# First experts of a two-layer attention and mixture-of-experts kernel: 176 inner columns split 128 and 48, with the 48 of two blocks turned and multiplied together

## The chip, the cores and the metric

The kernel runs on one core of a Trainium2 chip. The metric is the device time of one execution in microseconds; "time before" is the median over 14 executions. All arithmetic is in float32. Five engines work side by side, each on its own list of instructions: PE (TensorE, matrix products, with its weight loads shown apart as PEld), DVE (VectorE), ACT (ScalarE), POOL (GpSimd) and SP (which only issues transfers here). A matrix product has a stationary operand, which is loaded into the array (a LDWEIGHTS record), and a moving operand, whose columns stream through it (a MATMUL record). In float32 each product is recorded as two passes, two LDWEIGHTS and two MATMUL; a transposition through PE is one pass.

## What is computed

The input x has 32 sequences of 56 rows of 256 numbers, so 1792 tokens; the context has 32 x 1500 rows of 256. Four residual layers follow one another, each on the normalised x: a decayed scan over the context whose projected mean is added and normalised; a mixture of 16 experts; an attention over the context with a mask; a mixture of two experts with 1024 inner columns. The change is in the second of them:

```python
MOE_D = 176; E = 16; K = 6
scores = softmax(h @ gate_w.T); topk_w, topk_idx = top_k(scores, K)
for e in range(E):
    g = h @ w_gate[e].T            # [T, 176]
    u = h @ w_up[e].T              # [T, 176]
    out = silu(g) * u @ w_down[e].T
    y = y + cw[:, e:e + 1] * out   # cw: the weights of the six chosen experts
```

## The kernel before

The tokens are first sorted by expert: the 1792 tokens with six experts each become at most 99 blocks (`NB0`) of 128 rows, every block with rows of one expert only. The table `ei` holds for each block where its expert's weights begin in `w0_sb`, `idx` holds which rows of the normalised input `xn0` belong to the block, and `wgt` the gate weight of each row. All weights of the 16 experts lie in SBUF as `w0_sb`, [128, 16, 1216]: for each expert two slabs of gate and up columns (one for each half of the 256 input columns, 352 columns each) and then two slabs of 256 columns for the down product. The 176 inner columns are cut into two halves of 88 (`H0`), so each down slab fills partitions 0 to 87. `w0_down_pieces` (lines 188 to 203) yields the transfers that put the down weights there, 26 in all; they are issued on SP during the first layer.

`expert_blocks` (lines 704 to 772) serves both mixtures: the 99 blocks of the first with one unit each (`nq` = 1), and later the 15 blocks of the second with four units each. It is a software pipeline over t, written out by hand, and its order is the order of each engine's list (the schedule is manual for all engines in this stage). In iteration t:

1. `gate_up(t)`: two products of the turned rows `xT[t]` with the gate and up columns of the block's expert, 352 columns wide, into a PSUM tile `gu` (line 720); PE reads the expert's offset from `ei` first (line 715). Then ACT computes silu of the gate half into `sg` (line 726), and DVE multiplies it by the row's gate weight and by the up half into `hs` (line 732).
2. `turn(t-1)`: two transpositions of `hs`, 88 columns each, into a PSUM tile `tp` (line 738); DVE copies both to `hT` (line 740).
3. `turned_rows` for block t+1: two transpositions of the gathered rows `xb` (line 166), and a copy on ACT to `xT` (line 168). The rows were gathered by POOL four blocks ahead (line 865).
4. `down(t-2)`: two products of `hT` with the two down slabs, 256 columns wide, summed in a PSUM tile `y` (line 747); then `done` copies `y` on ACT to `yb` (line 873) and sends it from SP to the table `ys0` in HBM (line 874).
5. `side(t)`: small work of the neighbouring layers. For t from 2 to 21 three DVE instructions each that work out where each token's results will lie (lines 889 to 904); five context loads of 1.5 MB and five zero fills on SP; gathers of finished rows on POOL; and in four iterations four transpositions on PE for the first queries of the attention (line 840).

So gate-up of iteration t+1 needs the `xT` copied in iteration t, and the work of step 4 stands between the two in PE's list. The PSUM tiles have two buffers each, the SBUF tiles `sg`, `hs`, `hT`, `xT` and `yb` three.

After the stage, the attention begins. It scores with line 1027, whose operands use 32 partitions each, and sums with line 1075.

Of the kernel before, what the change touches and what calls it, by code (L numbers as in the profile page):

```python
# [8 lines left out]
F32 = mybir.dt.float32  # L9
# [45 lines left out]
def xattn_ffn_kernel(  # L55
# [132 lines left out]
    def w0_down_pieces():  # L188

        half = E0 // 2  # L190
        for e in range(half):
            for c in range(2):
                r = 0
                while r < H0:
                    f = e * F0 + c * H0 + r
                    n = min(H0 - r, P - f % P)
# [504 lines left out]
        V.tensor_copy(wgt, bl[:, P : P + NB0])  # L701
        V.tensor_copy(ei, ep[0:1, 0:P])

    def expert_blocks(nb, nq, f, w, ei, wk, ptr, pgu, pht, py, rows_of, done, ahead, wgt=None, side=None):

        fp = f // nq
        h = fp // 2
        doff = 2 * KD * fp
        piece = doff + 2 * D
        units = [(i, u) for i in range(nb) for u in range(nq)]  # L710
        xT, at, hs, hT, y = {}, {}, {}, {}, {}

        def gate_up(i, u):
            if u == 0:
                at[i] = PE.value_load(
                    ei[0:1, i : i + 1], min_val=0, max_val=w.shape[1] - nq * piece
                )
            gu = pgu.tile([P, 512], F32, tag="gu", name="gu")
            for k in range(KD):
                PE.matmul(  # L720
                    gu[:, 0 : 2 * fp], lhsT=xT[i][:, k, :],
                    rhs=w[:, bass.ds(at[i] + (u * piece + k * 2 * fp), 2 * fp)],
                    start=(k == 0), stop=(k == KD - 1),
                )
# [4 lines left out]
            if wgt is None:  # L729
                V.tensor_tensor(hs[i, u], sg, up, ALU.mult)  # L730
            else:
                V.scalar_tensor_tensor(hs[i, u], sg, wgt[:, i : i + 1], up, ALU.mult, ALU.mult)  # L732

        def turn(i, u):
            tp = pht.tile([P, 512], F32, tag="ht", name="tp")
            a = hs.pop((i, u))
            for c in range(2):
                PE.transpose(tp[0:h, c * P : (c + 1) * P], a[:, c * h : (c + 1) * h], ident)  # L738
            hT[i, u] = wk.tile([h, 2 * P], F32, tag="hT", name="hT")
            V.tensor_copy(hT[i, u], tp[0:h, 0 : 2 * P])  # L740

        def down(i, u):
            if u == 0:
                y[i] = py.tile([P, 512], F32, tag="y", name="y")
            a = hT.pop((i, u))
            for c in range(2):
                PE.matmul(  # L747
                    y[i][:, 0:D], lhsT=a[:, c * P : (c + 1) * P],
                    rhs=w[0:h, bass.ds(at[i] + (u * piece + doff + c * D), D)],
                    start=(u == 0 and c == 0), stop=(u == nq - 1 and c == 1),  # L750
                )
# [5 lines left out]
        if side:  # L757
            side(-1)
        for t in range(len(units) + 2):
            if t < len(units):  # L760
                gate_up(*units[t])
            if 0 <= t - 1 < len(units):
                turn(*units[t - 1])
            if t < len(units) and units[t][1] == nq // 2 and units[t][0] + 1 < nb:
                i = units[t][0] + 1
                if i + ahead - 1 < nb:
                    xb[i + ahead - 1] = rows_of(i + ahead - 1)
                xT[i] = turned_rows(wk, ptr, "tr", xb.pop(i))
            if t >= 2:
                down(*units[t - 2])  # L770
            if side:
                side(t)

    def levels_of(p):

# [74 lines left out]
    with tc.manual_schedule(  # L850
# [113 lines left out]
    with tc.manual_schedule(  # L964
# [255 lines left out]
        def turn(p, n):  # L1220
            return [transposed(2 * p + h, n) for h in range(2)]
# [77 lines left out]
    with tc.tile_pool(name="f1", bufs=3) as wk, tc.tile_pool(  # L1299
        name="f1_tr", bufs=2, space=PSUM  # L1300
    ) as ptr, tc.tile_pool(name="f1_gu", bufs=2, space=PSUM) as pgu, tc.tile_pool(
        name="f1_ht", bufs=2, space=PSUM
    ) as pht, tc.tile_pool(name="f1_y", bufs=2, space=PSUM) as py:
        last = NP - GP

        def side1(t):

            if t == -1:
                roots(mvs[NP - 1])
                sort_norm(NP - 1, mvs.pop(NP - 1))  # L1310
# [23 lines left out]
        expert_blocks(  # L1334
            NB1, NQ1, F1, w1_sb.rearrange("p e w -> p (e w)"), e1i,
            wk, ptr, pgu, pht, py, lambda i: xb1[i][:, 0:D], done1, 1, None, side1,
        )


# [54 lines left out]
```

## Time and profile before

| what | value |
|---|---|
| median of 14 executions | 894.48 us (891.03 to 907.58) |
| the profiled execution: its time, its span | 901.24 us, 899.5 us |
| mean granted TensorE clock | 0.948 |
| PE busy | 811.7 us, 90% of the span |
| DVE, ACT, POOL busy | 483.9, 343.3, 398.0 us |
| first experts, 209.70 to 462.40 us | PE busy 251.67 of 252.70 us, DVE 92.03, ACT 109.42, POOL 138.63 |
| attention, 466.80 to 704.10 us | PE busy 212.12 of 237.30 us, DVE 187.20 |
| second experts, 717.00 to 895.00 us | PE busy 174.27 of 178.00 us |

The stage times are read from windows of the trace. A row of the timeline gives the start, the length, the engine, the line, the operation and the operands' names and shapes; "88*128" is 88 rows (partitions) by 128 columns of the stationary operand. Equal instructions that touch are merged into one row, with their count behind x. The end of a matrix pass is modelled by the profiler, and passes overlap: what a pass really takes is seen from the distance between starts. Queue rows (SPq, PEldq) are instructions that only issue or read a register.

### The profile page before, as it was taken

To read this page: it belongs to the slowest core of one execution; us is meant where nothing else is said; L and a number is where in the kernel's file an instruction comes from. 1 tells how busy PE (TensorE), PEld (TensorE's weight loads), DVE (VectorE), ACT (ScalarE), POOL (GpSimd) and SP (SyncE) were. 2 spreads that over 40 slices of the span, in tenths; PEclk is the share of its full clock that TensorE was granted. 3 is DMA by queue.
4 is the path that set the end of the run, shared out by engine and by line. 5 is a ranking of instruction groups with operands and counts; after the bars stand their busy time and mean duration, and the time that the engine had idled before them with its cause. 6 is when DMAs were issued, how large, how long until landed. Compare 5 with 4: busy or idle time off the path is not lost.

```text
span 899.5 us, 18673 instructions
## 1 busy us (share of the span) xinstructions
PE 811.7 (90%) x6664; PEld 531.8 (59%) x6664; DVE 483.9 (54%) x1420; ACT 343.3 (38%) x901; POOL 398.0 (44%) x479
## 2 busy tenths in 40 slices
PE   4688788788999999999988999988959989999997
PEld 3345555545777777777754666555635556666664
DVE  3577777862552424322257989868739333333222
ACT  0233333312444444444435776746536321111110
POOL 4555655434347656575624655565540330111110
PEclk9799999958999999999988999998989999999999
DMA  8999999922987534344537988796963820011110
GB/s 250 351 390 384 379 368 355 305 65 74 313 295 247 161 106 141 101 141 116 125 106 249 305 273 279 244 309 232 320 232 93 274 83 13 25 35 30 35 31 17
DMA packets 77820, 176.58 MB, mean 196 GB/s; under 512 B 7795, under 2 KB 41476, under 8 KB 77732
## 3 DMA queue, kind: packets, MB, share of 16 engines
q1 hardware_dynamic: 64756, 139.55, 44.8%
q0 software_dynamic: 12976, 35.85, 14.2%
q8 instruction: 56, 0.92, 0.4%
q14 instruction: 32, 0.26, 0.1%
HBM read 150.83 MB, written 25.20 MB: 196 GB/s over the span
## 4 chain that ended last, share of the span: by engine, by line
PE 46%; POOL 11%; DMA 9%; issue 6%; DVE 3%; ACT 1%; POOLq 0%; DVEq 0%; ACTq 0%
PE gu L720 23%; PE y L747 14%; DMA g<-ys,back 8%; POOL g L782 6%; PE tp L738 4%; PE tp L166 3%; POOL g L792 2%; PE op L1075 1%; DVE cT L988 1%; POOL g L793 1%; POOL g L794 1%; DMA xs<-pay,to 1%; PE sp L1027 1%; POOL xr L795 1%; POOL xs L1166 0%
## 5 line engine op out<-in xcount | busy, mean ns | idle before, releaser
L720 PE MATMUL gu<-w_sb,xT 128*128 x396 | 136.3, 466 | 2.1 <-DMA xb<-xn,idx 1.1
L726 ACT ACTIVATE sg<-gu 128x176 f32<-128x176 f32 (+1 forms) x159 | 54.4, 343 | 216.9 <-PE gu L720 216.9
L865 POOL DMA_INDIRECT xb<-xn,idx x99 | 93.8, 947 | 91.8 <-PE tp L166 74.6
L732 DVE SCALAR_TENSOR_TENSOR hs<-sg,wgt,gu 128x176 f32<-128x176 f32 x99 | 39.3, 397 | 160.0 <-ACT sg L726 153.9
L720 PE MATMUL gu<-ring,xT 128*128 x240 | 114.3, 600 | 0.5 <-ACT xT L168 0.5
L782 POOL DMA_INDIRECT g<-ys,back x96 | 91.2, 950 | 33.3 <-issue 26.4
L747 PE MATMUL y<-w_sb,hT 88*128 x396 | 101.8, 379 | 0.0
L1027 PE MATMUL sp<-cT,xq 32*64 32x384 f32 x2048 | 94.1, 512 | 3.4 <-DVE cT L988 3.3
L720 PEld LDWEIGHTS gu<-w_sb,xT 128*128 128x128 f32 x396 | 75.0, 191 | 30.2 <-ACT xT L168 3.2
L730 DVE TENSOR_TENSOR hs<-sg,gu 128x256 f32<-128x256 f32 x60 | 25.2, 421 | 117.1 <-ACT sg L726 117.1
L738 PEld LDWEIGHTS tp<-ident,hs 128*88 128x88 f32 (+1 forms) x318 | 41.2, 130 | 62.9 <-issue 48.6
L988 DVE STREAM_TRANSPOSE cT<-ring 128x1536 f32<-128x1536 f32 x40 | 69.2, 1758 | 15.1 <-PE sp L1027 10.0
L1075 PE MATMUL op<-ring,pT 128*64 128x256 f32 x480 | 67.7, 396 | 9.4 <-issue 9.3
L1329 POOL DMA_INDIRECT out<-ob,ti x15 | 14.8, 989 | 130.9 <-DVE ob L1326 130.6
L1027 PEld LDWEIGHTS sp<-cT,xq 32*64 32x64 f32 x2048 | 45.7, 139 | 44.0 <-issue 17.5
L747 PEld LDWEIGHTS y<-w_sb,hT 88*128 88x128 f32 x396 | 67.3, 190 | 5.6 <-issue 0.2
L168 ACT COPY xT<-tp 128x256 f32<-128x256 f32 x130 | 48.4, 372 | 51.5 <-PE tp L166 50.6
L740 DVE COPY hT<-tp 88x256 f32<-88x256 f32 (+1 forms) x159 | 66.0, 415 | 0.7 <-PE tp L738 0.6
L720 PEld LDWEIGHTS gu<-ring,xT 128*128 128x128 f32 x240 | 45.6, 191 | 33.2 <-issue 29.5
L738 PE MATMUL tp<-ident,hs 128*88 128x128 f32 (+1 forms) x318 | 61.1, 274 | 2.6 <-DVE hs L730 2.6
L1075 PEld LDWEIGHTS op<-ring,pT 128*64 128x64 f32 x480 | 41.6, 142 | 36.9 <-issue 17.2
L747 PE MATMUL y<-ring,hT 128*128 x240 | 61.7, 380 | 0.0
(264 smaller groups left out, 1342.2 us busy)
## 6 DMA issues: line engine op xcount, KB each, us to landing
ring<-in_cx SPq DMA_DIRECT2D x52, 1536.0 KB
extra<-in_cx SPq DMA_DIRECT2D x12, 1536.0 KB
ys<-yb SPq DMA_DIRECT2D x99, 128.0 KB
xs<-zrow SPq DMA_DIRECT2D x5, 771.0 KB
mu<-in_mask SPq DMA_DIRECT2D x16, 187.5 KB
w_sb<-in_wg SPq DMA_DIRECT2D x2, 1408.0 KB
w_sb<-in_wu SPq DMA_DIRECT2D x2, 1408.0 KB
xn<-xn SPq DMA_DIRECT2D x16, 128.0 KB
```

The costliest lines, as they stand in the source:

```text
L168: A.copy(xT.rearrange("p k c -> p (k c)"), tp[:, 0 : KD * P])
L720: PE.matmul(gu[:, 0 : 2 * fp], lhsT=xT[i][:, k, :], rhs=w[:, bass.ds(at[i] + (u * piece + k * 2 * fp), 2 * fp)], start=(k == 0), stop=(k = ...
L726: A.activation(sg, gu[:, 0:fp], AF.Silu)
L732: V.scalar_tensor_tensor(hs[i, u], sg, wgt[:, i : i + 1], up, ALU.mult, ALU.mult)
L738: PE.transpose(tp[0:h, c * P : (c + 1) * P], a[:, c * h : (c + 1) * h], ident)
L740: V.tensor_copy(hT[i, u], tp[0:h, 0 : 2 * P])
L747: PE.matmul(y[i][:, 0:D], lhsT=a[:, c * P : (c + 1) * P], rhs=w[0:h, bass.ds(at[i] + (u * piece + doff + c * D), D)], start=(u == 0 and c ...
L782: G.indirect_dma_start(out=g[:, k, :], out_offset=None, in_=ys0[0 : n * P, :], in_offset=bass.IndirectOffsetOnAxis(ap=back[:, p, 3 * i + k ...
L865: G.indirect_dma_start(out=xb, out_offset=None, in_=xn0, in_offset=bass.IndirectOffsetOnAxis(ap=idx[:, i : i + 1], axis=0),)
L988: V.transpose(out=cT.rearrange("p j e q -> p j (e q)"), in_=slots[b % NS][:, :, P * n : P * n + P],)
L1027: PE.matmul(sps[a][64 * h : 64 * h + 64, 0 : Q * NCH], lhsT=xq[Q * a : Q * a + Q, e, 64 * h : 64 * h + 64], rhs=cTs[e // 4][h][Q * a : Q * ...
L1075: PE.matmul(op[64 * h : 64 * h + 64, 0:D], lhsT=pT[:, j, 64 * h : 64 * h + 64], rhs=slots[(2 * p + h) % NS][:, j, :], start=(j == 0), stop ...
```

## The change

The 176 inner columns are now split 128 and 48 (`R0`). The first down slab fills all 128 partitions, the second only partitions 0 to 47; the pieces that load them become 25. The first mixture gets a pipeline of its own, `first_blocks`; `expert_blocks` loses its weight argument and serves only the second.

In `first_blocks` DVE writes the weighted product in two instructions: 128 columns to `hs` and 48 to `rest`. One `rest` tile belongs to two successive blocks: the even block's 48 columns stand at column 0, the odd block's at column 64, with zeros (written once by POOL) between. `turn` transposes `hs` for every block; after an odd block it also transposes the 112 columns of `rest`, so that the even block's part lands on partitions 0 to 47 and the odd block's on 64 to 111, copied to `h2`. `down` of an even block makes only the product over its 128 rows. `down` of an odd block makes its own product over 128 rows, then one of 48 rows for the even block, from partition 0, and one of 48 rows for itself, from partition 64; then both blocks are done. The weights for the partitions from 64 are a copy of the odd block's second slab: SP reads the expert's offset and sends 48 KB from `w0_sb` to a tile `w2`, four blocks ahead of the block's gate-up. Block 98 has no partner and makes its 48-row product alone.

```diff
-H0 = F0 // 2
+R0 = F0 - P
+    def first_blocks(w, wk, ptr, pgu, pht, py, rows_of, done, ahead, side):
+        rest = [wk.tile([P, 64 + R0], F32, tag=f"rest{i}", bufs=1, name="rest") for i in range(3)]
+        def gate_up(i):
...
+            b = 64 * (i % 2)
+            for dst, o, n in ((hs[i], 0, P), (rest[i // 2 % 3][:, b : b + R0], P, R0)):
+                V.scalar_tensor_tensor(
+                    dst, sg[:, o : o + n], wgt[:, i : i + 1], gu[:, F0 + o : F0 + o + n],
+                    ALU.mult, ALU.mult,
+                )
+        def pair(i):
+            if i % 2 == 0 and i < NB0 - 1:
+                return []
+            return [(j, 64 * (j % 2)) for j in range(i - i % 2, i + 1)]
+        def rest_of_weights(i):
+            r = nc.sync.value_load(ei[0:1, i : i + 1], min_val=0, max_val=w.shape[1] - W0)
+            w2[i] = wk.tile([P, D], F32, tag="w2", bufs=4, name="w2")
+            nc.sync.dma_start(
+                out=w2[i][64 : 64 + R0, :], in_=w[0:R0, bass.ds(r + (2 * KD * F0 + D), D)]
+            )
+        def turn(i):
+            tp = pht.tile([P, 512], F32, tag="ht", name="tp")
+            PE.transpose(tp[:, 0:P], hs.pop(i), ident)
+            n = 64 * len(pair(i)) - 64 + R0
+            if pair(i):
+                PE.transpose(tp[0:n, P : 2 * P], rest[i // 2 % 3][:, 0:n], ident)
+            h1[i] = wk.tile([P, P], F32, tag="h1", name="h1")
+            V.tensor_copy(h1[i], tp[:, 0:P])
+            if pair(i):
+                h2[i] = wk.tile([P, P], F32, tag="h2", bufs=2, name="h2")
+                V.tensor_copy(h2[i][0:n, :], tp[0:n, P : 2 * P])
+        def down(i):
+            y[i] = py.tile([P, 512], F32, tag="y", name="y")
+            PE.matmul(
+                y[i][:, 0:D], lhsT=h1.pop(i), rhs=w[:, bass.ds(at[i] + 2 * KD * F0, D)],
+                start=True, stop=False,
+            )
+            for j, b in pair(i):
+                PE.matmul(
+                    y[j][:, 0:D], lhsT=h2[i][b : b + R0, :],
+                    rhs=w2.pop(j)[b : b + R0, :] if b
+                    else w[0:R0, bass.ds(at[j] + (2 * KD * F0 + D), D)],
+                    start=False, stop=True,
+                )
+            for j, _ in pair(i):
+                done(j, y.pop(j))
+        for i in (1, 3):
+            rest_of_weights(i)
+        for r in rest:
+            G.memset(r[:, R0:64], 0.0)
+        xT[0] = turned_rows(wk, ptr, "tr", xb.pop(0))
+        for t in range(NB0 + 2):
+            if t < NB0:
+                gate_up(t)
+                if t % 2 and t + 4 < NB0:
+                    rest_of_weights(t + 4)
+            if 0 < t <= NB0:
+                turn(t - 1)
+            if t + 1 < NB0:
...
+                xT[t + 1] = turned_rows(wk, ptr, "tr", xb.pop(t + 1))
+            if t >= 2:
+                down(t - 2)
+            side(t)
...
-        expert_blocks(
-            NB0, 1, F0, w0_sb.rearrange("p e w -> p (e w)"), ei,
-            wk, ptr, pgu, pht, py, rows_of, done, 4, wgt, side,
+        first_blocks(
+            w0_sb.rearrange("p e w -> p (e w)"), wk, ptr, pgu, pht, py, rows_of, done, 4, side,
         )
```

More of the change, by code (lines that the diff above doesn't have):

```diff
@@ L193, in w0_down_pieces @@
                 r = 0
-                while r < H0:
-                    f = e * F0 + c * H0 + r
-                    n = min(H0 - r, P - f % P)
+                while r < (R0 if c else P):
+                    f = e * F0 + c * P + r
+                    n = min((R0 if c else P) - r, P - f % P)
                     o = 2 * KD * F0 + c * D
@@ L702, in xattn_ffn_kernel @@
         V.tensor_copy(ei, ep[0:1, 0:P])
-    def expert_blocks(nb, nq, f, w, ei, wk, ptr, pgu, pht, py, rows_of, done, ahead, wgt=None, side=None):
+    def first_blocks(w, wk, ptr, pgu, pht, py, rows_of, done, ahead, side):
+        xT, at, hs, h1, h2, w2, y = {}, {}, {}, {}, {}, {}, {}
+        rest = [wk.tile([P, 64 + R0], F32, tag=f"rest{i}", bufs=1, name="rest") for i in range(3)]
+        def gate_up(i):
+            at[i] = PE.value_load(ei[0:1, i : i + 1], min_val=0, max_val=w.shape[1] - W0)
+            gu = pgu.tile([P, 512], F32, tag="gu", name="gu")
+            for k in range(KD):
+                PE.matmul(
+                    gu[:, 0 : 2 * F0], lhsT=xT[i][:, k, :],
+                    rhs=w[:, bass.ds(at[i] + k * 2 * F0, 2 * F0)],
+                    start=(k == 0), stop=(k == KD - 1),
+                )
+            sg = wk.tile([P, F0], F32, tag="sg", name="sg")
+            A.activation(sg, gu[:, 0:F0], AF.Silu)
+            hs[i] = wk.tile([P, P], F32, tag="hs", name="hs")
+            b = 64 * (i % 2)
[32 more added lines that the diff above has]
+            for j, b in pair(i):
+                PE.matmul(
+                    y[j][:, 0:D], lhsT=h2[i][b : b + R0, :],
+                    rhs=w2.pop(j)[b : b + R0, :] if b
+                    else w[0:R0, bass.ds(at[j] + (2 * KD * F0 + D), D)],
+                    start=False, stop=True,
+                )
+            for j, _ in pair(i):
+                done(j, y.pop(j))
+        xb = {i: rows_of(i) for i in range(ahead)}
+        for i in (1, 3):
[11 more added lines that the diff above has]
+            if t + 1 < NB0:
+                if t + ahead < NB0:
+                    xb[t + ahead] = rows_of(t + ahead)
+                xT[t + 1] = turned_rows(wk, ptr, "tr", xb.pop(t + 1))
+            if t >= 2:
+                down(t - 2)
+            side(t)
@@ L706, in expert_blocks @@
+    def expert_blocks(nb, nq, f, w, ei, wk, ptr, pgu, pht, py, rows_of, done, ahead, side):
         fp = f // nq
@@ L728, in gate_up @@
             up = gu[:, fp : 2 * fp]
[L729 to L732, printed above, removed]
+            V.tensor_tensor(hs[i, u], sg, up, ALU.mult)
         def turn(i, u):
@@ L756, in expert_blocks @@
         xT[0] = turned_rows(wk, ptr, "tr", xb.pop(0))
-        if side:
-            side(-1)
+        side(-1)
         for t in range(len(units) + 2):
@@ L770, in expert_blocks @@
                 down(*units[t - 2])
-            if side:
-                side(t)
+            side(t)
     def levels_of(p):
@@ L1335, in xattn_ffn_kernel @@
             NB1, NQ1, F1, w1_sb.rearrange("p e w -> p (e w)"), e1i,
-            wk, ptr, pgu, pht, py, lambda i: xb1[i][:, 0:D], done1, 1, None, side1,
+            wk, ptr, pgu, pht, py, lambda i: xb1[i][:, 0:D], done1, 1, side1,
         )
```

## The prediction

> **What bounds the kernel now.** I read the page's costliest groups first, then windows over the stage, then the chain of waits inside it, then one iteration engine by engine.
>
> ```profile
> L720 PE MATMUL gu<-w_sb,xT 128*128 x396 | 136.3, 466 | 2.1 <-DMA xb<-xn,idx 1.1
> L747 PE MATMUL y<-w_sb,hT 88*128 x396 | 101.8, 379 | 0.0
> ```
>
> The two products of the stage are among PE's largest groups, and PE hardly idles before them. A window of 60 us in mid-stage has PE busy all the time at full clock:
>
> ```profile
> 300.00:360.00 60.00, 60.00 (x298) 45.70 (x297) 22.49 (x77) 28.78 (x76) 37.33 (x40) 1.00 0.45 132
> ```
>
> (Columns: PE, PEld, DVE, ACT, POOL, clock, DMA share, GB/s.) The chain gives one iteration as the bare sum of PE's passes:
>
> ```profile
> 264.43 1.19 PE gu L720 x4
> 265.61 0.22 PE tp L738 x2
> 265.83 0.22 PE tp L166 x2
> 266.05 0.86 PE y L747 x4
> 266.91 1.19 PE gu L720 x4
> ```
>
> 1.19 + 0.22 + 0.22 + 0.86 = 2.49 us a block: a gate-up pass takes 0.296, a transposition 0.11, a down pass 0.216. But a second path has the same length. The timelines of PE, PEld and ACT over the same iteration (here by start of record):
>
> ```profile
> 264.26 1.35 PE L720 MATMUL gu<-w_sb,xT 128*128 x4
> 265.67 0.38 PE L166 MATMUL tp<-ident,xb 128*128 128x128 f32 x2
> 265.88 1.03 PE L747 MATMUL y<-w_sb,hT 88*128 x4
> 266.14 0.37 ACT L168 COPY xT<-tp 128x256 f32<-128x256 f32 x1 [0.17 <-PE tp L166]
> 266.56 0.97 PEld L720 LDWEIGHTS gu<-w_sb,xT 128*128 128x128 f32 x4
> 266.75 1.35 PE L720 MATMUL gu<-w_sb,xT 128*128 x4
> ```
>
> The row transpositions start 1.41 after the gate-up. From there to the next gate-up's weight load are 0.89 (265.67 to 266.56): transpose, hand over to ACT, copy 0.37, hand back. ACT idles 0.17 before the copy, so it is latency, not load. The load of 0.19 ends at 266.75, exactly when the four down passes are through. The down passes cover the turning of the next block's rows, with almost nothing to spare.
>
> **The change, part by part**, per pair of blocks, against 2 x 2.487 = 4.974.
>
> *Removed.* One transposition in four: -0.11, in the odd iteration (it turns an even block). The down passes stay eight of 256 columns per pair: four over 128 rows, four over 48.
>
> *Moved.* The even block's second product goes to the next iteration. So iterations with t even run two down passes after the row transpositions, 0.43 instead of 0.87, and PE then waits for `xT`. What is late next is that copy: 1.41 + 0.89 = 2.30 to the load, and the load's own share in front of the first pass. Upper bound of that share 0.19, its recorded length; a lower one comes from line 473 below, where four 16-column passes with a load each go by in 0.55, so at most 0.14 together; I take 0.10. Even iteration 2.40, -0.09. Two down passes fewer therefore bring a fifth of their 0.43.
>
> *Added.* Two 48-row products from partitions 0 and 64. Can they run at once? The trace of before has no 64-row operands, but line 1027 has 32-row ones, into separate PSUM tiles as here, and line 435 has a 3-row one between 128-row neighbours:
>
> ```profile
> 510.20 5.42 PE L1027 MATMUL sp<-cT,xq 32*64 32x384 f32 x128
> 515.55 0.43 PE L1075 MATMUL op<-ring,pT 128*64 128x256 f32 x1
> ...
> 102.70 0.62 PE L473 MATMUL lp<-gw_sb,xT 128*128 128x16 f32 x4 [0.46 <-ACT xT L168]
> 103.25 0.69 PE L435 MATMUL bp<-sm,takes 3*128 3x256 f32 x2
> 103.87 0.64 PE L294 MATMUL acc<-ring,cz 128*32 128x256 f32 x8
> ...
> 26.33 1.10 PE L332 MATMUL vp<-wout_sb,bcol 128*128 128x256 f32 x4 [0.60 <-DVE t L345]
> 27.36 0.69 PE L336 MATMUL vp<-bout_sb,ones 1*128 1x256 f32 x2
> 27.99 0.27 PE L348 MATMUL tk<-ident,t 128*3 128x128 f32 x1
> ```
>
> 128 passes of 384 columns pass in 5.35 us, 0.042 each; a lone one would take 0.216 x 384/256 = 0.32. So eight tiles of the array work together, and both passes of each: I take the two products as concurrent, 0.43 for four passes. But each change of tile shape costs. Line 435's two passes hold the array 0.62 to the next group, line 336's 0.63, where two down passes take 0.43: 0.19 to 0.20 more, a gap of some 0.09 and an uncovered load of 0.10 for one change. Neighbouring lines of equal shape (720, 738, 166, 747) show no gap. The pair changes shape twice, into the 48-row products and back to gate-up: 2 x 0.19 = 0.38. So 0.43 + 0.38 = 0.81 stands where four passes took 0.87. Bounds: 0.43 (no price) to 0.87 + 0.38 = 1.25 (not concurrent).
>
> The Trainium skill, page "TensorE: Matmul & The Clock Gate", Part 3, prices packed tiles at one product's duration plus some 4 ns for each further tile and lets a load for another row group overlap running products; by that the four passes would cost 0.43 and the sum below would be a gain of about 9 us. Its page "TensorEngine Tiling (Array Packing)", Key Properties, says that changing the mode drains the engine, without a price; the rows of lines 435 and 336 side with this one.
>
> Odd iteration: 1.19 + 0.11 + 0.22 + 0.43 + 0.81 = 2.76, +0.27. Its `xT` is ready after 1.19 + 0.11 + 0.89 = 2.19, well before.
>
> *Other engines.* DVE writes two pieces instead of one (397 ns for 176 columns; each piece between 0.14, its smallest rows, and 0.40) and copies 128 columns per block and again per pair (413 ns for 256; about half each). That is 0.2 to 0.5 us more per iteration. Around 240 us, with the three side instructions, DVE still idles 0.76 per iteration before line 732, and iterations do not get shorter than 2.40; `hs` has over an iteration until it is turned. Nothing. ACT makes the two `yb` copies of a pair together, 0.74, at the start of the even iteration; silu waits for gate-up's end 1.39 in. Nothing. They use the three `yb` buffers faster; before, ACT waited for one transfer once, 0.9 us. SP gets 49 more loads of the offset (PE's takes 0.30 to 1.15) and 48 KB transfers, before the `ys` issues and context loads of their iteration; SP's largest waits are for ACT's `yb` (219.7 us), and a weight copy has six iterations, 14 us, while gathers of 128 KB land in 2.7 to 5.4. Bounds 0 to 1 us in all, taken as 0. POOL's three small fills come after the first four gathers, and 25 pieces replace 26: nothing.
>
> *Sum.* Pair -0.09 + 0.27 = +0.18; 48 pairs with a following gate-up: +8.8 (0.184 unrounded). The query transpositions (line 840, 0.44 us after the down passes) fall twice into an even iteration's hole of 0.3: -0.6. The last blocks drop four-pass groups and add three changes of shape: +0.2. Total **+8.5 us**. What follows the stage starts from its last `ys0` block and moves with it. The profiled execution took 901.24 for a span of 899.5, 0.8% above the median 894.48; its iterations of 2.49 at full clock have no reason to differ in other executions, so I add to both: 909.7 for a profile like this one, **903** for the median.
>
> **The rivals.**
>
> *A. As above, slower by about 1%.* For it: lines 435, 336 and the equal lengths of the two paths. Between 899 and 910, from 0.1 to 0.33 a pair.
>
> *B. Faster: 64-row tiles join without a price.* The weight loads overlap and no gap opens. Odd iteration 1.95 + 0.43 = 2.38; pair 2.40 + 2.38 = 4.78, -0.19; 48 pairs -9: **885**. It decides once a change costs under 0.095 us (half the 0.19 of line 435). For it: no 64-row operand was seen. Against it: every change of shape above, from 1 to 32 rows and in both directions.
>
> *C. The two products don't run together.* The change then does not do what it says. Odd iteration +0.43: pair +0.61, 48 pairs +30: **924**; with only one pass of each overlapped +0.40, +19: **914**. For it: each product's two passes stand next to each other in PE's list. Against it: so they do in line 1027.
>
> *D. No change.* A change costs about 0.10, say because the load is hidden and only the gap stays: pair about 0: **895**.
>
> **How the numbers follow.** A 0.64, B 0.15, C 0.11, D 0.10. The time is A's, 903. About 0.5%, 4.5 us, is what a measurement of this kernel can tell from no change: 890 to 899. A's low edge touches that. Faster: B, 0.15 and a little of D, so 0.17; same: 0.08 of D and 0.05 of A, 0.13; slower: 0.70. The range has to hold 8 in 10: A and D, and half of C and B's edge: 889 to 914. A's own is 899 to 910.
>
> **What would show it.** In the profile after: PE's weight load of `gu` waits for ACT's `xT` some 48 times, 0.3 to 0.4 each, where before it did so 4 times; iterations alternate, 2.40 and 2.76; the 48-row products are two pairs of simultaneous passes, 0.32 and 0.22 long, with about 0.3 between the last 128-row pass and the first of them instead of 0.22; the stage takes about 261 us instead of 252.7. Alternating 2.40 and 2.38 is B; 48-row passes in single file are C. Wrong altogether I would be if DVE or the 48 KB copies held PE back, which would show as waits of lines 738 or 747.

## The result, and the profile after

| | before | after |
|---|---|---|
| median | 895.58 us (889.94 to 907.58, 47 executions) | 904.83 us (902.82 to 914.59, 10 executions) |
| the profiled execution: time, span, clock | 901.24, 899.5, 0.948 | 901.80, 900.1, 0.961 |
| first gate-up of the first experts to the issue of the last `ys0` block | 209.7 to 462.8: 253.1 us | 208.9 to 469.2: 260.3 us |

The changed kernel is slower: ratio 1.0122, 95% interval 1.0098 to 1.0147, the medians 9.25 us apart. (Here and below the medians are over all executions, and the ratios leave out those in a slower state.) The two profiled executions must not be subtracted: the one of before lay 0.6% above its median and the one of after 0.3% below, and the attention, which the change doesn't touch, took 236.7 us from its first to its last scores instruction in the one and 232.8 in the other, with the clock's half-speed stretches at other places. The stage itself can be compared, and it is 7.2 us longer.

The costliest groups of the stage, after (line, engine, operation, operands, count; then busy time and the mean of one in ns; then idle time before them and what ended most of it):

```profile
L714 PE MATMUL gu<-w_sb,xT 128*128 x396 | 144.4, 487 | 4.6 <-ACT xT L168 2.0
L714 PEld LDWEIGHTS gu<-w_sb,xT 128*128 128x128 f32 x396 | 67.6, 190 | 60.4 <-ACT xT L168 23.1
L757 PE MATMUL y<-w_sb,h 128*128 x198 | 59.3, 381 | 0.5 <-ACT yb L956 0.5
```

The gate-up's weight load now idles 60.4 us before it starts, and 23.1 of that ends with ACT's copy of `xT`. PE shows little idle time of its own, since a load record and the modelled end of the pass before it cover the gap. The waits of the stage name it directly (us in total, times, longest), first in the kernel before:

```profile
PEld gu L720 <- ACT xT L168: 3.2, 4, 1.3
```

and after:

```profile
PEld gu L714 <- ACT xT L168: 23.1, 47, 1.5
PEld gu L714 <- issue: 16.6, 50, 0.4
PEld y L762 <- issue: 16.2, 49, 0.3
...
ACT yb L956 <- DMA ys<-yb: 2.2, 2, 1.7
```

47 gate-ups wait for `xT`, mostly for 0.43 us, where four did before. In the other iterations, some 50 times each, the load before the first 48-row product and the load before the gate-up that follows idle 0.3 "for issue", that is for nothing the profile names: these two start 0.31 after the start of the last pass before them, where the load of a 128-row pass starts while the pass before it runs. The chain of waits through one odd and one even iteration (start, length, what):

```profile
264.29 1.45 PE gu L714 x4
265.74 0.11 PE tp L745
265.85 0.22 PE tp L166 x2
266.07 0.43 PE y L757 x2
266.50 0.63 PE y L762 x4
267.13 1.38 PE gu L714 x4
268.51 0.11 PE tp L745
268.62 0.11 PE tp L748
268.73 0.22 PE tp L166 x2
268.95 0.43 PE y L757 x2
269.38 0.03 issue
269.41 1.45 PE gu L714 x4
```

Where before had one repeated sum of PE's passes, a hand-over ("issue", after the wait for ACT) now sits in every second iteration, and the gate-up's four passes are put down as 1.38 and 1.45 in place of 1.19, because the chain counts in an uncovered load among them (0.10) and the idle stretch ahead of them. In the timelines of PE, PEld and ACT the same stretch shows where each pass and load begins:

```profile
265.90 0.60 PE L757 MATMUL y<-w_sb,h 128*128 x2
266.43 0.48 PE L762 MATMUL y<-w_sb,h 48*128 x1
266.44 0.48 PE L762 MATMUL y<-w,h 48*128 48x256 f32 x1
266.75 0.38 PE L762 MATMUL y<-w_sb,h 48*128 x1
266.76 0.38 PE L762 MATMUL y<-w,h 48*128 48x256 f32 x1
267.06 1.45 PE L714 MATMUL gu<-w_sb,xT 128*128 x4
...
267.06 0.89 PEld L714 LDWEIGHTS gu<-w_sb,xT 128*128 128x128 f32 x4 [0.33 <-issue]
...
269.41 0.59 PEld L714 LDWEIGHTS gu<-w_sb,xT 128*128 128x128 f32 x3 [0.43 <-ACT xT L168]
...
268.99 0.37 ACT L168 COPY xT<-tp 128x256 f32<-128x256 f32 x1
```

The two 48-row products start 0.01 apart, and so do their second passes: they do run together. But the first of them begins 0.31 after the last 128-row pass instead of 0.22, the second pair 0.32 after the first, and the gate-up 0.31 after the second. In the even iteration the load of the gate-up starts at 269.41, 0.05 after the copy that ended at 269.36. An iteration is from here on the distance between the starts of two gate-ups' first passes: 267.06 to 269.41, 2.35 us, is the even one; the odd one before it took 2.77. Over the whole stage the medians are 2.349 and 2.775, so 5.124 a pair against 4.976 before.

The stage's 7.2 us can be added up from the starts of all gate-ups and the end: 48 pairs at +0.148 are +7.1; two even iterations (t = 10 and t = 16) were longer by 1.0 together; the four iterations with query transpositions, and the two that follow them, took 1.06 more than normal instead of 1.76, -0.7; the end, from the last gate-up to the last `ys0` issue, took 6.3 instead of 5.1, +1.2; and the first pair took 5.80 instead of 7.16, -1.4. That is +7.2. The last term is the clock's and not the change's: in the profile of before the second gate-up, too, ran at half speed (granted clock 0.53 from 213 to 216 us, against 1.00 from 212.4 to 214 us in the profile after).

```profile
213.32 2.68 PE L720 MATMUL gu<-w_sb,xT 128*128 x4 [0.46 <-ACT xT L168]
```

```profile
212.43 1.45 PE L714 MATMUL gu<-w_sb,xT 128*128 x4 [0.46 <-ACT xT L168]
```

These rows of the timelines of before and of after are the gate-up of t = 1. Without that accident the stage would be 8.6 us longer, close to the distance of the medians. The ratio's interval, 8.8 to 13.2 us of 895.58, begins just above that and allows up to 4.6 us more; where that would lie, I did not find.

### The profile page after: what moved, and what is told of

Its sections match the earlier page's. It is cut to its first block, busy times and chain, and to the rows that moved or that the text cites. A ratio compares the mean times of both kernels' runs of the same rounds, so it can differ in the third digit from the quotient of the medians.

```text
span 900.1 us, 18919 instructions
## 1 busy us (share of the span) xinstructions
PE 808.9 (90%) x6615; PEld 494.8 (55%) x6615; DVE 489.8 (54%) x1569; ACT 339.1 (38%) x901; POOL 398.7 (44%) x482
## 4 chain that ended last, share of the span: by engine, by line
PE 50%; issue 5%; DVE 5%; POOL 5%; DMA 4%; ACT 2%; POOLq 0%; DVEq 0%
PE gu L714 13%; PE gu L808 9%; PE sp L1109 5%; PE y L832 5%; PE op L1157 4%; PE y L757 4%; PE y L762 3%; DMA g<-ys,back 3%; DVE cT L1070 2%; PE tp L166 2%; POOL g L865 2%; PE tp L1149 1%; PE tp L823 1%; PE tp L745 1%; DVE sc L1122 1%
## 5 line engine op out<-in xcount | busy, mean ns | idle before, releaser
L714 PE MATMUL gu<-w_sb,xT 128*128 x396 | 144.4, 487 | 4.6 <-ACT xT L168 2.0
L724 DVE SCALAR_TENSOR_TENSOR hs<-sg,wgt,gu 128x128 f32<-128x128 f32 x99 | 34.4, 348 | 158.7 <-ACT sg L720 150.9
L714 PEld LDWEIGHTS gu<-w_sb,xT 128*128 128x128 f32 x396 | 67.6, 190 | 60.4 <-ACT xT L168 23.1
L814 ACT ACTIVATE sg<-gu 128x256 f32<-128x256 f32 x60 | 22.9, 384 | 138.1 <-PE gu L808 138.1
L720 ACT ACTIVATE sg<-gu 128x176 f32<-128x176 f32 x99 | 31.5, 318 | 110.4 <-PE gu L714 106.2
L757 PE MATMUL y<-w_sb,h 128*128 x198 | 59.3, 381 | 0.5 <-ACT yb L956 0.5
L875 POOL TENSOR_TENSOR g<-g 128x768 f32<-128x768 f32 x16 | 29.2, 1828 | 61.0 <-DMA g<-ys,back 60.9
L294 PE MATMUL acc<-ring,cz 128*32 128x256 f32 x768 | 54.2, 440 | 0.3 <-DVE cz L270 0.3
L544 POOL TENSOR_SCALAR oh<-iota,off 128x128 f32<-128x128 f32 x64 | 39.7, 634 | 16.4 <-DVE off L520 14.1
```

What stands on the lines that cost most here:

```text
L294: PE.matmul(acc[Q * g : Q * g + Q, 0:D], lhsT=cz[:, j, 1 - h : 1 - h + Q], rhs=c[:, j, :], start=(h == 0 and m == 0), stop=(h == 1 and m = ...
L544: G.tensor_scalar(oh[:, i, :], iota, off[:, i : i + 1], None, ALU.is_equal)
L714: PE.matmul(gu[:, 0 : 2 * F0], lhsT=xT[i][:, k, :], rhs=w[:, bass.ds(at[i] + k * 2 * F0, 2 * F0)], start=(k == 0), stop=(k == KD - 1),)
L757: PE.matmul(y[i][:, 0:D], lhsT=h1.pop(i), rhs=w[:, bass.ds(at[i] + 2 * KD * F0, D)], start=True, stop=False,)
```

## The experiments

Three of the chips on which the experiments ran took 967 to 970 us for the kernel before, a fourth 964, not 895, and there PE, ACT and DVE stop for some microseconds five times in this stage (last section). The whole times below therefore carry these stops. Their cost is given as the time that the iterations from the first to the last gate-up take above their normal length, added up: 27 to 49 us, against 4 and 3 us in the two profiles of the first chip, where nothing stops. What an edit does to the work is read from the median length of the iterations, which agrees to 0.002 us between kernels and chips wherever the same work is done.

My theory: the pair is longer because (a) the even iteration, freed of two passes, runs into the wait for `xT`, and (b) the joint products pay two changes of tile shape. The rivals: the joint products are not joint, or the loss comes from the new DVE instructions, the weight copies or `yb`.

**Rows turned earlier, in the changed kernel** (rows_two_ahead). If the hole is the wait for `xT`, it closes when the rows are turned two iterations ahead.

```diff
-        xT[0] = turned_rows(wk, ptr, "tr", xb.pop(0))
+        for i in range(2):
+            xT[i] = turned_rows(wk, ptr, "tr", xb.pop(i))
...
-            if t + 1 < NB0:
-                if t + ahead < NB0:
-                    xb[t + ahead] = rows_of(t + ahead)
-                xT[t + 1] = turned_rows(wk, ptr, "tr", xb.pop(t + 1))
+            if t + ahead < NB0:
+                xb[t + ahead] = rows_of(t + ahead)
+            if t + 2 < NB0:
+                xT[t + 2] = turned_rows(wk, ptr, "tr", xb.pop(t + 2))
...
-            w0_sb.rearrange("p e w -> p (e w)"), wk, ptr, pgu, pht, py, rows_of, done, 4, side,
+            w0_sb.rearrange("p e w -> p (e w)"), wk, ptr, pgu, pht, py, rows_of, done, 5, side,
```

> The changed kernel, but each block's rows are turned two iterations before their gate-up instead of one (five gathers ahead instead of four), so the copy to xT is never awaited. Theory (even iterations have a hole while the copy is awaited, and the changes of tile shape use up what the joint 48-row products save): the even iteration falls from 2.35 to its passes, 1.19 + 0.22 + 0.22 + 0.43 = 2.06, the odd one stays 2.78; pair 4.84 against 5.12, 48 pairs -14 us against the changed kernel, so about 5 us faster than the kernel before (ratio 0.993 to 0.996). Rival (the loss is DVE's, ACT's or SP's added work, or the changes of shape alone): no gain, ratio stays at 1.012.

Measured: even 2.159, odd 2.671, a pair 4.83. The chain of waits, from the end of an even iteration through an odd one:

```profile
258.80 0.43 PE y L757 x2
259.24 1.18 PE gu L714 x4
260.42 0.11 PE tp L745
260.53 0.22 PE tp L166 x2
260.75 0.43 PE y L757 x2
261.18 0.63 PE y L762 x4
261.81 1.38 PE gu L714 x4
```

There is no "issue" any more, the gate-up after an even iteration's products is back at 1.18, and only the one after the 48-row products keeps 1.38. So the hole is worth 5.124 - 4.830 = 0.294 a pair, in the two forms of a late load (0.19 in the even iteration) and an uncovered one (0.10 in the odd). The whole time, 968.52 us, is 1.0024 of before on the same chip (0.9978 to 1.0071): the gain of 7 us that 49 pairs at -0.146 would make does not show. The stops took 40 us here, and 32 us on the same chip in before_rows_two_ahead (below), whose iterations are those of the kernel before. A difference of this size would hide the gain, but the kernel before itself has no trace on this chip.

**The same beside the changed kernel** (rows_two_ahead_again, changed_again). To weigh the hole in time, both ran on one chip.

> The changed kernel with its rows turned two iterations ahead, a second time: in the first run its iterations were 2.16 and 2.67, pair 4.83 as expected, but on that chip every engine stopped together for some 8 us about every 40 us, in the kernel before as well, so that the time couldn't be told. Theory, without such stops: 48 x 0.29 = 14 us faster than the changed kernel, ratio to before 0.993 to 0.996. Rival: 1.012 as the changed kernel.

> The changed kernel itself, beside the others on the same chip. Ratio 1.010 to 1.015; iterations 2.35 and 2.78.

Measured: 969.12 us (1.0037 of before, 0.9992 to 1.0083) with the rows turned earlier; the changed kernel as it is 984.93 (1.0184, 1.0117 to 1.0251), with the same 2.349 and 2.775 as on the first chip. The stops were equal in the two, 40.0 and 40.4 us, so the 15.8 us between them can be set against the hole, 49 x 0.294 = 14.4. The expectation for the changed kernel (1.010 to 1.015) was too low; the stops were longer than those of the two kernels made from before (27 and 32 us, on another chip).

**Rows turned earlier, in the kernel before** (before_rows_two_ahead). If that edit were a gain by itself, the reading above would be worth less. The same lead of two iterations in `expert_blocks`, for the first mixture alone, again with five gathers ahead:

```diff
-        xT[0] = turned_rows(wk, ptr, "tr", xb.pop(0))
+        lead = 2 if nq == 1 else 1
+        for i in range(lead):
+            xT[i] = turned_rows(wk, ptr, "tr", xb.pop(i))
...
-                xT[i] = turned_rows(wk, ptr, "tr", xb.pop(i))
+                i += lead - 1
+                if i < nb:
+                    xT[i] = turned_rows(wk, ptr, "tr", xb.pop(i))
...
-            wk, ptr, pgu, pht, py, rows_of, done, 4, wgt, side,
+            wk, ptr, pgu, pht, py, rows_of, done, 5, wgt, side,
```

> The kernel before with the same early turning of the rows in the first experts. Theory: PE's passes alone already fill its iterations of 2.487, so nothing moves, ratio 0.998 to 1.002. Rival (turning the rows early is a gain of its own, whatever the change): faster by as much as the changed kernel with it.

Measured: every iteration 2.488, and 965.37 us, 1.0020 of before (0.9971 to 1.0069). In the kernel before nothing waits for `xT`, as predicted; the path has the length of the passes and no more.

**The hole alone** (before_moved). The kernel before with nothing changed but the place of the even block's second product: still 88 rows, no shape changes, no weight copies, no further DVE instructions.

```diff
-            for c in range(2):
+            late = nq == 1 and i % 2 == 0 and i < nb - 1
+            todo = [(i, 0)] if late else [(i, 0), (i, 1)]
+            if nq == 1 and i % 2:
+                todo = [(i, 0), (i - 1, 1), (i, 1)]
+            for j, c in todo:
...
-            if u == nq - 1:
-                done(i, y.pop(i))
+            if u == nq - 1 and not late:
+                for j in ([i - 1, i] if nq == 1 and i % 2 else [i]):
+                    done(j, y.pop(j))
...
```

> The kernel before (176 = 88 + 88, all as it was), but the second down product of an even block is made in the next iteration, so that iterations have two and six down passes in turn. PE's passes are the same. Theory: the even iteration waits for xT, 2.35 to 2.40 instead of falling to 2.05, the odd one is 2.49 + 0.43 = 2.92; pair 5.27 to 5.32 against 4.97, 49 pairs +15 to +17 us, ratio 1.016 to 1.019. Rival (the waiting for xT is covered, moving passes costs nothing): ratio 1.000.

Measured: even 2.248, odd 3.022, a pair 5.27, +0.294: the same figure that the rows turned earlier gave back. The even iteration is 0.10 shorter and the odd one 0.10 longer than expected, since from start to start the uncovered load behind the hole counts to the odd one. 985.15 us, 1.0153 of before (1.0028 to 1.0279). The chain has the same hand-over without any 48-row product:

```profile
257.40 0.03 issue
257.42 1.45 PE gu L720 x4
...
259.31 1.30 PE y L751 x6
260.61 1.19 PE gu L720 x4
```

So moving work out of the iteration is the whole of (a). In the changed kernel the joint products and the dropped transposition then give back 0.146 of it.

**The 48-row products without a change of shape** (whole_shape_rest). Both products over 112 rows, with the partner's rows of the weights filled with zeros, so the array keeps its whole shape and the two can't run together.

```diff
+        for lo, hi in ((32, 64), (64, P)):
+            G.memset(w0_sb[lo:hi, :, 2 * KD * F0 + D : W0], 0.0)
...
+        N = 64 + R0
...
-                    y[j][:, 0:D], lhsT=h2[i][b : b + R0, :],
-                    rhs=w2.pop(j)[b : b + R0, :] if b
-                    else w[0:R0, bass.ds(at[j] + (2 * KD * F0 + D), D)],
+                    y[j][:, 0:D], lhsT=h2[i][0:N, :],
+                    rhs=w2.pop(j)[0:N, :] if b
+                    else w[0:N, bass.ds(at[j] + (2 * KD * F0 + D), D)],
...
+        for i in range(4):
+            V.memset(w2s[i][0:64, :], 0.0)
```

> The changed kernel, but its two 48-row products are made over 112 rows, with zeros in the weights for the partner's rows, so that no tile shape changes and nothing runs together: four passes in a row. Theory: the odd iteration is 1.19 + 0.11 + 0.22 + 0.43 + 0.87 = 2.82 instead of 2.78, the even one stays 2.35: 2 us slower than the changed kernel, ratio to before 1.013 to 1.016; joining the products with its two changes of shape is worth only 0.04 us a pair. Rival (the changes of shape are the loss): back to the kernel before, ratio 1.000.

Measured: even 2.248, odd 2.914, a pair 5.16; 983.49 us, 1.0144 of before (1.0026 to 1.0262). The pair is what was expected (2.35 + 2.82), with 0.10 of it in the other iteration: no change of shape puts an uncovered load into the even one.

```profile
256.40 0.43 PE y L762 x2
256.83 0.87 PE y L767 x4
257.70 1.19 PE gu L719 x4
```

Four passes in single file take 0.87 and the gate-up behind them 1.19, where the joint ones take 0.63 with a gate-up of 1.38 behind them. 0.87 + 1.19 = 2.06 against 0.63 + 1.38 = 2.01: running the two products at once brings 0.04 to 0.05 us a pair, not the 0.43 of two passes. The two changes of shape take the rest, 0.39, so 0.19 each.

**Both products from one row group** (one_row_group). The opposite bound: the changed kernel with both 48-row products on partitions 0 to 47. It leaves out the odd block's rest, so its result is not the layer's; only its times are used.

```diff
-                    y[j][:, 0:D], lhsT=h2[i][b : b + R0, :],
-                    rhs=w2.pop(j)[b : b + R0, :] if b
-                    else w[0:R0, bass.ds(at[j] + (2 * KD * F0 + D), D)],
+                    y[j][:, 0:D], lhsT=h2[i][0:R0, :],
+                    rhs=w[0:R0, bass.ds(at[j] + (2 * KD * F0 + D), D)],
```

> The changed kernel, but both 48-row products read partitions 0 to 47, so they can't run together; the odd block's rest is thereby left out and the even block's multiplied in its place. The changes of tile shape stay. Theory (the two products of the changed kernel do run together): four passes in a row, the odd iteration 2.78 + 0.43 = 3.21, the even one 2.35, pair 5.56, 49 pairs 21 us slower than the changed kernel, ratio to before about 1.035. Rival (they never ran together, or it doesn't matter): the same as the changed kernel.

Measured: even 2.350, odd 3.200; 1002.01 us, 1.0314 of before (1.0247 to 1.0380). The timeline of PE:

```profile
230.52 1.13 PE L762 MATMUL y<-w_sb,h 48*128 x4
231.57 1.15 PE L714 MATMUL gu<-w_sb,xT 128*128 x3
```

The four passes now begin at 230.52, 230.84, 231.05 and 231.27, and the gate-up 1.06 after the first of them, where with the joint ones it begins 0.63 after. The odd iteration is 0.425 longer, two passes of 0.216: this is what the second row group saves. The pair, 5.549, is 0.388 longer than the 5.161 of whole_shape_rest, which makes the same number of passes in single file: that is the price of the two changes of shape, with no joining in it. The rival "not joint" is out.

**Balanced, whole shape** (balanced_whole_shape). Each block's rest, over 112 rows, in the next block's iteration, so that every iteration has four down passes again and the one transposition in four is still saved. The edit is shown against whole_shape_rest.

```diff
-            for j, b in pair(i):
+            todo = ([(i - 1, 64 * ((i - 1) % 2))] if i else []) + ([(i, 0)] if i == NB0 - 1 else [])
+            for j, b in todo:
                 PE.matmul(
-                    y[j][:, 0:D], lhsT=h2[i][0:N, :],
+                    y[j][:, 0:D], lhsT=h2[min(j | 1, NB0 - 1)][0:N, :],
...
-            for j, _ in pair(i):
+            for j, _ in todo:
                 done(j, y.pop(j))
```

> The changed kernel with its 48-row products made over 112 rows (weights padded with zeros, so no change of tile shape), and each block's product made in the iteration of the next block, so that every iteration has four down passes, as before. Theory: no hole and no change of shape; what stays of the change is one transposition in four: 2.38 and 2.49, pair 4.87 against 4.97 before, 49 pairs -5 us, ratio 0.993 to 0.996. Rival (the turning of the rest, its copies on DVE, and the weight copies by SP cost something by themselves): ratio 1.000 or more.

Measured: 2.489 and 2.381, a pair 4.87, as expected: the hole is gone without turning rows earlier, and the saved transposition (0.11) is all that is left of the change. The time missed its expectation: 978.86 us, 1.0150 of before (1.0084 to 1.0216), and the stops took 48 us.

**Five `yb` buffers** (two_ahead_buffers). Two even iterations of the changed kernel were longer because ACT waited for the transfers out of `yb`; the stops might have been the same thing. The rows turned earlier, with five `yb` buffers in place of three (and, not shown here, two `rest` tiles and three `w2` to make room):

```diff
-            yb = wk.tile([P, D], F32, tag="yb", name="yb")
+            yb = wk.tile([P, D], F32, tag="yb", bufs=5, name="yb")
```

> The changed kernel with its rows turned two iterations ahead and five instead of three buffers for yb (paid for by two instead of three tiles for the rest and three instead of four for the copied weights, fetched two blocks ahead). The iterations stay 2.16 and 2.67, and ACT no longer waits for the transfers of yb, which in the changed kernel lengthened two iterations by 1.0 us together. On the two chips of the earlier runs everything stopped five times in this stage, each time as the second half of a token group's results was being gathered. If those stops come from ACT's wait for yb, they shrink, and the ratio to before falls below 0.993; if they don't, it stays at 1.002 to 1.004 on such a chip, and 0.993 to 0.996 on one without stops.

Measured: iterations unchanged (2.158, 2.671), the stops still 36.5 us, 977.06 us, 1.0058 of before (1.0004 to 1.0111). In this stage ACT no longer waits for a transfer out of `yb`, where with three buffers it did so five times for 6.9 us in all (rows_two_ahead). The stops are not a lack of `yb` buffers.

**One change of shape for four blocks** (groups_of_four, and twice more on other chips). If 0.38 a pair goes into changes of shape, joining four blocks' 48-row products halves it. Blocks i and i+2 share a bank of PSUM, ACT copies two blocks at once, the rows are turned two iterations ahead.

```diff
-            y[i] = py.tile([P, 512], F32, tag="y", name="y")
+            if i % 4 < 2:
+                y[i] = py.tile([P, 512], F32, tag="y", name="y")
+            else:
+                y[i] = y[i - 2]
+            o = D * (i % 4 // 2)
...
-            for j, b in pair(i):
+            if i % 4 < 3 and i < NB0 - 1:
+                return
+            for j in range(i - i % 4, i + 1):
+                b = 64 * (j % 2)
+                o = D * (j % 4 // 2)
...
```

> Rows turned two iterations ahead, and the 48-row products collected over four blocks: two pairs at a time, one after the other, so that two changes of shape serve four blocks. PSUM: the products of blocks i and i+2 share a bank, ACT copies two blocks at once, the transposed rows have one bank. Theory: four blocks take 4 x 1.185 + 8 x 0.109 + 6 x 0.109 + 8 x 0.2165 + 4 x 0.2165 + 0.38 = 9.24 against 9.95 before; 24.5 groups -17 us, ratio 0.980 to 0.984, if nothing else becomes the bound; in the first 20 iterations DVE, with some 2.2 us of work per iteration, may. Rival (changes of shape cost nothing, only the hole did): no better than the rows turned ahead alone, 0.994.

> The groups of four again, in the hope of a chip without the stops. In the earlier run its iterations outside of them took 9.26 us for four blocks (9.24 expected, 9.95 before), but the stops took 16 us more than with the kernel before and its rows turned early. Without stops: 17 us faster than before, ratio 0.980 to 0.984. With them: 1.00 to 1.01 as before.

> The same kernel as groups_of_four, on whatever chip comes. Its four iterations together take 9.26 us at full clock, against 9.95 before (4 x 2.488); 24 such groups make 16.6 us less. If the chip is one on which the kernel before takes about 895 us and the stage has no stops of all engines, the time should be 0.980 to 0.985 of before. If the stops of 5 to 10 us are there as on the chips of the other runs (before at 967 to 970 us), they should cost this kernel some 49 us against some 33 before and take the gain away: 1.003 to 1.014.

Measured: the four iterations 2.054, 3.103, 2.158 and 1.945, together 9.26, on all three chips, against 9.95 before. The chain at the 48-row products:

```profile
261.72 0.43 PE y L761 x2
262.15 1.06 PE y L770 x8
263.22 1.38 PE gu L714 x4
```

Eight passes in 1.06 where two pairs of four take 1.26, and one gate-up of 1.38 for four blocks instead of two: the price of a change of shape is paid per visit, not per product. In time it lost on every chip: 971.82 us, 1.0051 (1.0003 to 1.0099); 983.19, 1.0131 (1.0078 to 1.0184); 971.65, 1.0077 (1.0040 to 1.0113). The stops took 48 to 49 us. So no version was faster than the kernel before in a measurement; that this one would where the stops are absent, by some 16 us (0.69 for each of 24 groups), is worked out from its iterations and was not measured.

## Why the prediction was right, point by point

**Forecast and result.** 903 was said, 904.83 came, and A, the likeliest case, is what happened. The sum of +8.5 stands against +7.2 in the profiled stage, +8.6 without the half-speed gate-up of before, and +9.25 between the medians. Some of that agreement is luck: the pairs cost 1.7 us less than said, the `yb` waits and the end 2.0 us more.

**Even iteration, said 2.40, measured 2.349.** The mechanism was right: 47 waits for ACT's `xT` were found where 48 were forecast. The term that was mis-sized is the 0.89 from the first row transposition to the next gate-up's load: it took 0.84 (268.57 to 269.41), because ACT's copy began 0.42 after the transposition and not 0.47. It did so in nearly all even iterations, and 0.47 after in the odd ones; why, the runs don't show. The 0.10 for a load was right in size and stands in another place. The first pass is recorded as starting with its load, so the load behind the hole falls to the odd iteration (0.40 between the first two passes from 269.41, instead of 0.295). The even iteration has the like at its own start, after the change of shape (267.06 to 267.46): without shape changes it is 2.248, with them 2.349.

**Odd iteration, said 2.76, measured 2.775.** The 0.81 for the joint passes was 0.83: a gap of 0.09 and an uncovered load of 0.105 at each of the two changes, 0.195 against the 0.19 read from line 435. Part of it stands elsewhere than I put it: the load after the second change is counted in the even iteration, and in return the load after the hole in the odd one.

**The pair, said +0.18, measured +0.148.** 48 pairs, +7.1 instead of +8.8. before_moved and rows_two_ahead split it: +0.294 by the hole, -0.146 by the joint products and the dropped transposition, which is 0.11 of it. The joint products as such are worth 0.04.

**Queries, said -0.6, measured -0.7.** They fall into the holes twice, as forecast, and the iteration behind each hole is 0.10 shorter, since its load is then covered.

**The tail, said +0.2, measured +1.2; `yb` waits, 0 taken of 0 to 1, measured 1.0.** The second, and part of the first, are the same thing: ACT copies two `yb` in a row after an odd iteration, with three buffers. In the timeline of ACT around t = 10

```profile
235.38 0.37 ACT L956 COPY yb<-y 128x256 f32<-128x256 f32 x1 [0.63 <-PE y L762]
237.43 0.37 ACT L956 COPY yb<-y 128x256 f32<-128x256 f32 x1 [1.67 <-DMA ys<-yb]
...
237.90 0.38 ACT L168 COPY xT<-tp 128x256 f32<-128x256 f32 x1
```

the second copy waits 1.67 for a transfer, the silu and the `xT` copy queue behind it, and the even iteration, which has no slack before `xT`, grows by 0.70. At the end block 98's products wait 0.50 for ACT's two copies of the pair before it, and before that, with only two passes to cover it, the load of the last transposition waits 0.54 for DVE's `hs` (0.16 in the kernel before). I had put the `yb` waits at the low end of their bounds and missed these two.

**DVE, the weight copies, the side work: nothing was said, and but for that wait at the end nothing was found.** PE idles 0.5 us before line 757 and 0.1 before line 745 in the whole stage.

**Rival B, no price for tile shapes.** The Trainium skill, page "TensorE: Matmul & The Clock Gate", Part 3, prices packed tiles at one product's duration and a few ns for each further tile. The starts agree with that between the tiles themselves (0.01 apart), but not with what stands around them: the odd iteration would be 2.38 and was 2.775. The page "TensorEngine Tiling (Array Packing)", Key Properties, says that a change of mode drains the array. That is the page these rows side with: they show a price of 0.195 us a change, with float32 loads of 128 columns, though not the draining as such.

**Rivals C and D.** C's 3.20 is what one_row_group shows, and the changed kernel does not. D asked for a change at 0.10; it is 0.195.

## What to carry to other kernels

Small products on separate row groups do run at once, but between whole-array products the pair of shape changes cost 0.39 us here, almost the 0.43 that joining two saved: collect more of them for each visit, or pad them to the whole shape, which cost only 0.04 us a pair more. Before moving work out of an iteration, look for a second path of the same length: what the passes covered (here the turning of the next block's rows) becomes the new wait, and is best begun an iteration earlier in the same edit. Where work is bunched on one engine every second iteration, its output buffers have to be counted for two.

## What the runs showed that I had not expected

On the chips of the experiments the kernel before took 964 to 970 us, not 895, and its relatives show why in part. Five times in the stage, at about iterations 23, 38, 54, 70 and 86, PE stands idle for 2 to 7 us, much of it together with ACT and DVE, and after most of these stops the granted clock is 0.5 for 3.4 to 10.2 us. Those places follow the gathers of finished rows for one token group each on POOL. The stage in windows (start and end; busy time of PE, PEld, DVE, ACT and POOL with counts; clock; DMA share; GB/s), with the rows turned earlier:

```profile
270.00:280.00 10.00, 5.24 (x18) 2.75 (x17) 1.39 (x6) 1.73 (x6) 5.70 (x7) 0.73 0.50 163
280.00:290.00 10.00, 10.00 (x38) 6.44 (x38) 2.92 (x14) 3.09 (x9) 4.18 (x4) 0.76 0.61 193
```

and of the changed kernel on the first chip, where there is nothing of the kind:

```profile
270.00:280.00 10.00, 9.94 (x46) 5.99 (x46) 3.22 (x14) 4.06 (x12) 7.56 (x9) 1.00 0.97 315
```

Within such a stop PE idles for nothing that the profile names, as in groups_of_four (ACT, too, then starts a silu only at 270.88, after 5.38 us of idling, though the gate-up that it reads had begun at 265.31):

```profile
267.25 1.35 PE L714 MATMUL gu<-w_sb,xT 128*128 x4
271.63 0.48 PE L745 MATMUL tp<-ident,hs 128*128 128x128 f32 x1 [3.04 <-issue]
...
276.38 0.69 PE L166 MATMUL tp<-ident,xb 128*128 128x128 f32 x2 [4.06 <-issue]
```

Added up over the stage, the time above normal iterations was 27 to 32 us for the three kernels before_moved, before_rows_two_ahead and whole_shape_rest and for one_row_group, 37 to 40 for the changed kernel and the ones with the rows turned earlier, 48 to 49 for groups_of_four and balanced_whole_shape. The distance from the first to the last gate-up was 276.0 with pairs of 4.98 (before_rows_two_ahead), 273.1 to 276.7 with pairs of 4.83, and 274.9 to 276.3 with pairs of 4.63, as if something else set the pace there; but balanced_whole_shape, with 4.87, took 286.8, which a common floor doesn't explain. What stops the engines, why only on some chips, and why some of these kernels lose more by it stays open. The attention, too, was longer there, 272 to 284 us from its first to its last scores instruction against 233 to 237.
